# An expert layer on one core: features formed turned, with the weights standing in the array

## The chip, the core and the metric

The kernel runs on one core of a Trainium2 chip. The core's engines work at the same time, each on its own queue of instructions in order: TensorE (PE in the profile; its weight loads are listed apart as PEld), VectorE (DVE), ScalarE (ACT), GpSimd (POOL), and SyncE (SP), whose queue here only starts transfers. ScalarE and GpSimd start transfers too. Transfers from all queues share the core's 16 DMA engines. Matmuls read their operands from SBUF and write to PSUM, which has eight banks of 512 f32 values on each of 128 partitions; SBUF is the larger on-chip memory.

A matmul has one operand that *stands* in TensorE's array (loaded by an LDWEIGHTS instruction) and one that *moves* through it, a column at a time. All data are f32. An ordinary f32 product shows in the profile as two weight loads and two matmuls, a transpose as one of each.

The metric is the time of one execution in device microseconds, as the median of several runs. The kernel before takes 764.09 us (runs of 763.78, 764.09 and 767.37).

## The reference

The input is x of 4 x 1024 tokens with 256 features, and a context of 77 rows for each of the four sequences. Cross-attention comes first, then a mixture of experts:

```python
def swiglu(x, w1, w2, w3):
    return jax.nn.silu(x @ w1) * (x @ w3) @ w2
...
scores = jax.nn.softmax(xf @ Wg, axis=-1)             # 4096 tokens, 32 experts
weights, indices = jax.lax.top_k(scores, TOP_K)       # 4 experts a token
...
for e in range(E):
    ...                                               # the tokens that chose e, at most C of them
    out = swiglu(xf[tok], W1[e], W2[e], W3[e]) * w[:, None]
    y = y.at[tok].add(out)
z = swiglu(xf, Ws1, Ws2, Ws3)                         # the shared expert, all tokens
return (y + z).reshape(B, S, D)
```

An expert has W1 and W3 of 256 x 128 and W2 of 128 x 256; the shared expert's hidden width is 256. The input is added to each of the two layers' results.

## The kernel before

**Stages.** After loading and preparing weights, the kernel runs attention over 32 tiles of 128 tokens (up to about 400 us), with the routing of each block of 512 tokens behind it. Each normalised token row, with its routing numbers, is scattered to a table `xr` in DRAM, once for each expert that the token chose. Then come the expert tiles (about 449 to 720 us), and a tail in which the results are gathered, added and stored.

**An expert tile** is 128 rows of one expert, taken from `xr`. There are 144 in this run, numbered j: 128 (`NM_`) in a main loop and 16 (two lots of eight, the number read at run time) in the body of a `tc.Switch`. Which expert a tile belongs to is only known at run time: a table in SBUF holds it, `registers` (line 1083) loads eight entries at a time into registers of an engine, and `ev[j]` is tile j's expert in TensorE's registers. All experts' weights lie in SBUF in one array `we`, 768 columns an expert: for each half k of the 256 inputs 128 columns of W1 and 128 of W3, and then 256 columns of W2.

**The steps of a tile** are four functions, `steps` in line 1249. In round j of the loop, `expert_in` runs for tile j, `expert_mid` for tile j-1, `expert_turn` for j-2 and `expert_out` for j-3:

- `expert_in` (L1156): two transposes on TensorE turn the rows (PSUM bank `pgT`), VectorE copies them to `gT`, inputs down, tokens across.
- `expert_mid` (L1165): for each k, `gT` stands and 256 columns of `we` move (W1 and W3 side by side), which gives the bank `peh`, tokens down and 2 x 128 features across. ScalarE takes the Silu of the first half to `h` (L1176), VectorE multiplies it by the second (L1177).
- `expert_turn` (L1180): a transpose on TensorE turns `h` (bank `phT`), and ScalarE copies it to `ehT` (L1184).
- `expert_out` (L1187): `ehT` stands, W2 moves, bank `py`; ScalarE scales the rows by their routing weights into `y` (L1196), and GpSimd scatters the 128 rows to their places in `ys` in DRAM (L1197).

**Work around the tiles.** `fetch` (L1101) brings eight tiles' rows on SP's queue, seven rounds ahead, and loads the registers. `take` (L1216) brings back, for 128 tokens, the four results each, once those are scattered, and `add_taken` adds them on VectorE, a step a round. The shared expert runs on blocks of 512 tokens, `shared_in` (two halves), `shared_mid`, `shared_out`, `shared_add` (L581 to L634), placed between the tiles and in the tail; a block's turned rows come from DRAM (`xnd`) by `fetch_shared` (L575) into a tile `sx` of 512 KB. In the tail, six `gather` calls of 1 MB each run on SP's queue (`gy`), and the blocks 3, 4 and 5 of the shared expert are done between the additions and stores.

**What sets the order.** Within `as_written` each engine's instructions keep the order of the program text; nothing is reordered between engines' queues by a planner. A tile pool with `bufs=n` gives a name n buffers in turn, and an instruction that writes a buffer waits until the readers of its previous contents are done. PSUM banks are handed out in turn from one pool of eight. The pool `bp` holds the expert tiles' buffers, two of each name unless said otherwise; `sxp` holds `sx`, three of them.

Of the kernel before, what the change touches and what calls it, by code (L numbers as in the profile page):

```python
# [9 lines left out]
F32 = mybir.dt.float32  # L10
I32 = mybir.dt.int32
U32 = mybir.dt.uint32
AF = mybir.ActivationFunctionType
# [17 lines left out]
def kernel(  # L31
# [65 lines left out]
    def bank(name):  # L97
        return ps.tile([P, 512], F32, tag="bank", name=name)
# [982 lines left out]
    sxp = ctx.enter_context(tc.tile_pool(name="sxp", bufs=3, side="right"))  # L1081
# [14 lines left out]
    ev, groups = [], {}  # L1096
# [4 lines left out]
    def fetch(j):  # L1101
# [10 lines left out]
        ev.extend(registers(e_tab, jt, mybir.EngineType.PE, NE - 1))  # L1112
        groups[j // RG] = [g]
# [41 lines left out]

    def expert_in(j, _):  # L1156
        g = groups[j // RG][0]
        pt = bank(f"pgT_{j}")
        for k in range(KC):
            nc.tensor.transpose(pt[:, k * P : (k + 1) * P], g[:, j % RG, k * P : (k + 1) * P], ident)  # L1160
        gT = bp.tile([P, KC, P], F32, tag="gT", name=f"gT_{j}")
        nc.vector.tensor_copy(gT.rearrange("p k t -> p (k t)"), pt[:, :D])  # L1162
        return gT

    def expert_mid(j, gT):  # L1165
        ph = bank(f"peh_{j}")
        for k in range(KC):
            nc.tensor.matmul(  # L1168
                ph[:, : 2 * H],
                gT[:, k, :],  # L1170
                we[:, ds(ev[j] * EW + k * 2 * H, 2 * H)],
                start=(k == 0),
                stop=(k == KC - 1),
            )
        h = bp.tile([P, H], F32, tag="h", name=f"h_{j}")
        nc.scalar.activation(h, ph[:, :H], AF.Silu)  # L1176
        nc.vector.tensor_tensor(h, ph[:, H : 2 * H], h, ALU.mult)  # L1177
        return h

    def expert_turn(j, h):  # L1180
        pt = bank(f"phT_{j}")
        nc.tensor.transpose(pt[:, :P], h, ident)  # L1182
        hT = bp.tile([P, P], F32, tag="ehT", name=f"ehT_{j}")
        nc.scalar.copy(hT, pt[:, :P])  # L1184
        return hT
# [63 lines left out]
    steps = [expert_in, expert_mid, expert_turn, expert_out]  # L1249
# [5 lines left out]
    with as_written():  # L1255
        fetch(0)
        fetch_shared(1, nc.sync)
        for j in range(NM_ + len(steps)):
            if j % RG == 1 and j + RG - 1 <= NM_:
                fetch(j + RG - 1)  # L1260
            if j in (4 * RG + 4, 5 * RG + 4, 6 * RG + 4):
                fetch_shared(j // RG - 2, nc.sync)
# [47 lines left out]
            if j == NM_ + 2:  # L1310
                fetch_shared(5, nc.scalar)
    assert not adds
    ahead = groups[NM_ // RG][0]
    for n in tc.Switch(more, (NJ - NM_) // RG + 1, hint="more"):
        end = NM_ + n * RG
# [3 lines left out]
        del ev[NM_ + RG :]  # L1319
# [135 lines left out]
```

## Time and profile before

| | |
|---|---|
| median of three runs | 764.09 us |
| the profiled execution | 762.74 us |
| its span, first to last instruction | 761.0 us |
| mean granted TensorE clock | 0.989 of full |
| TensorE matmul busy | 720.0 us |
| VectorE, ScalarE, GpSimd busy | 478.2, 402.3, 404.1 us |
| features `peh` (L1168): 576 matmuls | 150.7 us busy |
| output `py` (L1192): 288 matmuls | 86.1 us busy |
| turning the rows `pgT` (L1160): 288 | 55.1 us busy |
| turning the features `phT` (L1182): 144 | 39.3 us busy |
| bytes moved by DMA | 111.98 MB |

The span has 1.74 us around it that belong to the execution but to no instruction. A group of the profile has its line, engine, operation, what is written from what (`peh<-we,gT`), and the count; then the busy time of the group (overlaps counted once), the mean duration of one, and the idle time of its engine ahead of them with what ended it. Matmuls are pipelined: the mean duration of one `peh` matmul is 385 ns, while two of them start about 217 ns apart. Shapes are partitions x elements. In a timeline row, `x4` means four such instructions merged, the second column is from the first one's start to the last one's end, and brackets give idle time of the engine and what ended it. The slices are fortieths of the span, some 19 us each.

### The profile page before, as it was taken

The page shows a single profiled execution, that of the slowest core. Times are in us where ns is not written, and L with a number is a line of the kernel's source. Part 1 is how long each engine was busy: PE and PEld are TensorE (multiplying, and loading weights), DVE is VectorE, ACT ScalarE, POOL GpSimd, SP SyncE. Part 2 cuts the span into 40 slices and gives each one's busy share as a digit, 9 for nine tenths or more (in the row PEclk, how much of TensorE's full clock was granted, in tenths as well). Part 3 has the DMA queues.
Part 4 walks back from the last instruction along what each step waited for, and adds up shares of the span by engine and source line. Part 5 has one row for each costly group of instructions (what it writes and reads, how often), then busy time and mean ns, then how long its engine had stood idle before and what let it go on. Part 6 is the DMA issues. An engine that isn't in the chain of part 4 may idle for free. (4 is left out here: it accounts for less than half of the span.)

```text
span 761.0 us, 13078 instructions
## 1 busy us (share of the span) xinstructions
PE 720.0 (95%) x3515; PEld 536.6 (71%) x3515; DVE 478.2 (63%) x1368; ACT 402.3 (53%) x1730; POOL 404.1 (53%) x492
## 2 busy tenths in 40 slices
PE   7999999999999999999987779999999999999996
PEld 5866777677777767777763457788888887876754
DVE  2965565777877878776757433644545466645766
ACT  2658567666777576766553002455555555544310
POOL 1003343346777878777786655565565555553500
PEclk9999999999999999999998989999999999999999
DMA  8930000402217131513136451555746579847594
GB/s 284 342 113 1 1 1 1 132 7 87 100 59 253 47 127 52 170 59 120 74 97 210 140 189 65 159 173 183 224 161 195 166 262 311 258 127 244 186 342 163
DMA packets 78599, 111.98 MB, mean 147 GB/s; under 512 B 8949, under 2 KB 63667, under 8 KB 78515
## 3 DMA queue, kind: packets, MB, share of 16 engines
q1 hardware_dynamic: 60319, 68.76, 29.4%
q0 software_dynamic: 13056, 36.72, 13.0%
q10 hardware_dynamic: 5140, 5.55, 2.1%
q8 instruction: 32, 0.52, 0.3%
q14 instruction: 52, 0.43, 0.2%
HBM read 62.36 MB, written 48.64 MB: 146 GB/s over the span
## 5 line engine op out<-in xcount | busy, mean ns | idle before, releaser
L327 ACT ACTIVATE p<-sc,mx 128x77 f32<-128x77 f32 x512 | 159.5, 352 | 93.2 <-DVE mx L319 93.2
L1197 POOL DMA_INDIRECT ys<-y,place x144 | 138.9, 964 | 124.1 <-ACT y L1196 102.0
L1168 PE MATMUL peh<-we,gT 128*128 x576 | 150.7, 385 | 6.9 <-DVE gT L1162 5.4
L378 PE MATMUL po<-we,pT 128*128 128x256 f32 (+1 forms) x640 | 147.3, 383 | 4.8 <-DVE pT L365 3.4
L555 POOL DMA_INDIRECT xr<-xn,row x128 | 128.1, 1000 | 41.1 <-issue 33.1
L342 POOL TENSOR_TENSOR p<-p,su 128x385 f32<-128x385 f32 (+1 forms) x96 | 91.1, 974 | 97.5 <-DVE su L337 76.5
L311 PE MATMUL sc<-we,qT 128*128 128x385 f32 (+1 forms) x384 | 138.9, 509 | 0.9 <-POOL qT L297 0.9
L378 PEld LDWEIGHTS po<-we,pT 128*128 128x128 f32 (+1 forms) x640 | 118.4, 190 | 27.1 <-DVE pT L365 5.8
L327 ACT ACTIVATION_READ_ACCUMULATOR p<-sc,mx 128x1 f32 x512 | 119.3, 233 | 0.0
L1168 PEld LDWEIGHTS peh<-we,gT 128*128 128x128 f32 x576 | 99.2, 192 | 16.7 <-DVE gT L1162 6.5
L311 PEld LDWEIGHTS sc<-we,qT 128*128 128x128 f32 x384 | 71.1, 189 | 54.3 <-issue 27.7
L1176 ACT ACTIVATE h<-peh 128x128 f32<-128x128 f32 x144 | 40.0, 278 | 116.0 <-PE peh L1168 76.3
L1177 DVE TENSOR_TENSOR h<-peh,h 128x128 f32<-128x128 f32 x144 | 41.9, 291 | 87.1 <-ACT h L1176 80.2
L1192 PE MATMUL py<-we,ehT 128*128 x288 | 86.1, 381 | 0.0
L1196 ACT ACTIVATE y<-py,own 128x256 f32<-128x256 f32 x144 | 68.3, 475 | 17.8 <-PE py L1192 2.0
L319 DVE TENSOR_REDUCE mx<-sc 128x5 f32<-128x385 f32 (+1 forms) x96 | 54.3, 576 | 32.8 <-PE sc L311 30.1
L1162 DVE COPY gT<-pgT 128x256 f32<-128x256 f32 x144 | 60.5, 420 | 19.5 <-PE pgT L1160 9.1
L1160 PE MATMUL pgT<-ident,g 128*128 128x128 f32 x288 | 55.1, 274 | 1.3 <-DMA g<-xr 0.5
L1160 PEld LDWEIGHTS pgT<-ident,g 128*128 128x128 f32 x288 | 40.1, 142 | 17.2 <-issue 2.3
L1192 PEld LDWEIGHTS py<-we,ehT 128*128 128x128 f32 x288 | 43.6, 191 | 11.6 <-issue 0.8
L589 PE MATMUL ph<-sx,ws 128*128 128x512 f32 x96 | 46.0, 628 | 1.6 <-DVE y L1236 1.0
L360 PEld LDWEIGHTS pp<-ident,p 128*128 128x128 f32 x320 | 36.1, 139 | 11.4 <-issue 5.5
(227 smaller groups left out, 927.3 us busy)
## 6 DMA issues: line engine op xcount, KB each, us to landing
g<-xr SPq DMA_DIRECT2D x144, 136.0 KB
gx<-ys SPq DMA_DIRECT2D x20, 512.0 KB
gy<-ys SPq DMA_DIRECT2D x6, 1024.0 KB
xr<-y SPq DMA_DIRECT2D x1, 4352.0 KB
y<-in_x SPq DMA_DIRECT2D x8, 512.0 KB
xnd<-xnT SPq DMA_DIRECT2D x6, 512.0 KB
we<-in_W SPq DMA_DIRECT2D x8, 384.0 KB
out<-y ACTq DMA_DIRECT2D x12, 256.0 KB
```

Source lines behind the costliest of these rows:

```text
L311: nc.tensor.matmul(sc[:, : (h1 - h0) * SK], qTs[blk][:, k, o : o + P], mq[:, b, k, h0 * SK : h1 * SK], start=(k == 0), stop=(k == KC - 1),)
L319: nc.vector.tensor_reduce(mx[:, h0:h1], sv, AX.X, ALU.max, negate=True)
L327: nc.scalar.activation(probs[t][:, h, :], sv[:, h - h0, :], AF.Exp, bias=mx[:, h : h + 1], accum_out=su[:, h : h + 1],)
L342: nc.gpsimd.tensor_tensor(p[:, h0:h1, :], p[:, h0:h1, :], su[:, h0:h1].unsqueeze(2).to_broadcast([P, h1 - h0, SK]), ALU.mult,)
L378: nc.tensor.matmul(po[:, :D], pT[:n, i, :], vo[b][:n, i, :], start=(i == 0), stop=(i == KT - 1))
L555: sct = nc.gpsimd.indirect_dma_start(out=xr, out_offset=bass.IndirectOffsetOnAxis(ap=row[:, i : i + 1], axis=0), in_=xn[:, c, :], in_offse ...
L1160: nc.tensor.transpose(pt[:, k * P : (k + 1) * P], g[:, j % RG, k * P : (k + 1) * P], ident)
L1162: nc.vector.tensor_copy(gT.rearrange("p k t -> p (k t)"), pt[:, :D])
L1168: nc.tensor.matmul(ph[:, : 2 * H], gT[:, k, :], we[:, ds(ev[j] * EW + k * 2 * H, 2 * H)], start=(k == 0), stop=(k == KC - 1),)
L1192: nc.tensor.matmul(py[:, :D], hT, we[:, ds(ev[j] * EW + KC * 2 * H, D)], start=True, stop=True)
L1196: nc.scalar.activation(y, py[:, :D], AF.Identity, scale=own[:, i, 1:2])
L1197: sent = nc.gpsimd.indirect_dma_start(out=ys, out_offset=bass.IndirectOffsetOnAxis(ap=place_[:, i : i + 1], axis=0), in_=y, in_offset=None,)
```

## The change

The features are formed turned. In `expert_mid` the experts' weights now stand in the array, a block of 128 x 128 at a time, and `gT` moves: for each of W1 and W3 (f) and each half k of the inputs there is a product of 128 moving columns. The bank `peh` then holds features down and tokens across, W1's in columns 0 to 127 and W3's in 128 to 255. Silu and product therefore write `ehT` directly, and the transpose, the bank `phT`, its copy and the buffer `h` are gone; `ehT` has three buffers. The third step only passes its tile on, so the output of a tile stays in the same round.

The standing weights are read from a fixed place: a new function `weigh` copies the tile's 512 columns of W1 and W3 on ScalarE from `we`, at an offset from ScalarE's own registers (`eva`, loaded in `fetch` beside `ev`), to a tile `w` of two buffers. The first two tiles of the main loop and of the Switch body are copied in `expert_in`; every other tile's copy stands in `expert_mid` of the tile two before, behind the Silu. `last` keeps the main loop from copying for tiles of the Switch body. W2 is still read from `we` in `expert_out`.

To make room, `sxp` has two buffers instead of three, and the loads of the shared blocks move: block 4 is loaded where block 5 was (after the main loop, on ScalarE's queue), and block 5 in the tail, on ScalarE's queue behind `shared_in(3, 1)`.

```diff
-    sxp = ctx.enter_context(tc.tile_pool(name="sxp", bufs=3, side="right"))
+    sxp = ctx.enter_context(tc.tile_pool(name="sxp", bufs=2, side="right"))
...
         ev.extend(registers(e_tab, jt, mybir.EngineType.PE, NE - 1))
+        eva.extend(registers(e_tab, jt, mybir.EngineType.Activation, NE - 1))
...
+    fixed, last = {}, [NM_]
+
+    def weigh(j):
+
+        fixed[j] = bp.tile([P, KC * 2 * H], F32, tag="w", name=f"w_{j}")
+        nc.scalar.copy(fixed[j], we[:, ds(eva[j] * EW, KC * 2 * H)])
+
     def expert_in(j, _):
         g = groups[j // RG][0]
+        if j % NM_ < 2:
+            weigh(j)
...
     def expert_mid(j, gT):
+
+        w = fixed.pop(j)
         ph = bank(f"peh_{j}")
-        for k in range(KC):
-            nc.tensor.matmul(
-                ph[:, : 2 * H],
-                gT[:, k, :],
-                we[:, ds(ev[j] * EW + k * 2 * H, 2 * H)],
-                start=(k == 0),
-                stop=(k == KC - 1),
-            )
-        h = bp.tile([P, H], F32, tag="h", name=f"h_{j}")
-        nc.scalar.activation(h, ph[:, :H], AF.Silu)
-        nc.vector.tensor_tensor(h, ph[:, H : 2 * H], h, ALU.mult)
-        return h
-
-    def expert_turn(j, h):
-        pt = bank(f"phT_{j}")
-        nc.tensor.transpose(pt[:, :P], h, ident)
-        hT = bp.tile([P, P], F32, tag="ehT", name=f"ehT_{j}")
-        nc.scalar.copy(hT, pt[:, :P])
+        for f in range(2):
+            for k in range(KC):
+                nc.tensor.matmul(
+                    ph[:, f * P : (f + 1) * P],
+                    w[:, (2 * k + f) * H : (2 * k + f + 1) * H],
+                    gT[:, k, :],
+                    start=(k == 0),
+                    stop=(k == KC - 1),
+                )
+        hT = bp.tile([P, P], F32, tag="ehT", name=f"ehT_{j}", bufs=3)
+        nc.scalar.activation(hT, ph[:, :P], AF.Silu)
+        nc.vector.tensor_tensor(hT, ph[:, P : 2 * P], hT, ALU.mult)
+        if j + 2 < last[0]:
+            weigh(j + 2)
+        return hT
+
+    def expert_rest(j, hT):
+
         return hT
...
-    steps = [expert_in, expert_mid, expert_turn, expert_out]
+    steps = [expert_in, expert_mid, expert_rest, expert_out]
...
-            if j in (4 * RG + 4, 5 * RG + 4, 6 * RG + 4):
+            if j in (4 * RG + 4, 5 * RG + 4):
                 fetch_shared(j // RG - 2, nc.sync)
...
             if j == NM_ + 2:
-                fetch_shared(5, nc.scalar)
+                fetch_shared(4, nc.scalar)
...
-        end = NM_ + n * RG
+        end = last[0] = NM_ + n * RG
...
-        del ev[NM_ + RG :]
+        del ev[NM_ + RG :], eva[NM_ + RG :]
...
         shared_in(3, 1, AF.Silu)
+        fetch_shared(5, nc.scalar)
```

More of the change, by code (lines that the diff above doesn't have):

```diff
@@ L1095 @@
     bp = bp_stack.enter_context(tc.tile_pool(name="bp", bufs=2, reuse_waits="tile"))
-    ev, groups = [], {}
+    ev, eva, groups = [], [], {}
     def table(j):
```

## The prediction, made before the result was known

> **What bounds the kernel now.** I read the page's busy shares and slices first, to see which engine is the bound and where.
>
> ```profile
> span 761.0 us, 13078 instructions
> PE 720.0 (95%) x3515; PEld 536.6 (71%) x3515; DVE 478.2 (63%) x1368; ACT 402.3 (53%) x1730; POOL 404.1 (53%) x492
> PE   7999999999999999999987779999999999999996
> DMA  8930000402217131513136451555746579847594
> ```
>
> TensorE is busy 95% of the span, and nearly without a hole from slice 25 to slice 39; the expert tiles run in most of these (about 449 to 720 us). The DMA engines are close to full in slices 33 to 35 and again in slice 39, the tail. So time is won only by shortening TensorE's own work per tile, and it is kept only where no transfer ends last. Next the costliest groups, for what one expert tile issues (x144 tiles).
>
> ```profile
> L1168 PE MATMUL peh<-we,gT 128*128 x576 | 150.7, 385 | 6.9 <-DVE gT L1162 5.4
> L1176 ACT ACTIVATE h<-peh 128x128 f32<-128x128 f32 x144 | 40.0, 278 | 116.0 <-PE peh L1168 76.3
> L1196 ACT ACTIVATE y<-py,own 128x256 f32<-128x256 f32 x144 | 68.3, 475 | 17.8 <-PE py L1192 2.0
> L1160 PE MATMUL pgT<-ident,g 128*128 128x128 f32 x288 | 55.1, 274 | 1.3 <-DMA g<-xr 0.5
> ```
>
> An ordinary product in f32 is two weight loads and two matmuls (576 for 288 in the text), a transpose one of each (288 for 288). The idle column shows that TensorE hardly waits. What a step costs TensorE is not its mean duration, which overlaps the next, but the distance between starts. The chain of waits gives that, here in a stretch where it runs along TensorE.
>
> ```profile
> 709.70 0.87 PE peh L1168 x4
> 710.56 0.11 PE phT L1182
> 710.67 0.43 PE py L1192 x2
> 711.11 0.22 PE pgT L1160 x2
> 711.32 0.86 PE peh L1168 x4
> 712.19 0.11 PE phT L1182
> 712.30 0.43 PE py L1192 x2
> ```
>
> A tile takes 1.63 us: 0.87 for the features (peh), 0.11 for turning them (phT), 0.43 for the output (py), 0.22 for turning the rows (pgT). The same 1.63 us separates every two tiles in the timeline around 520 us. Features plus turn run 709.70 to 710.67 and 711.32 to 712.30: 0.97 and 0.98, mean 0.975.
>
> **TensorE's part of the change.** The turn goes: one transpose, 0.11 us. The four matmuls of 256 moving columns (0.217 us each) become eight of 128 moving columns, each with its own load of 128x128 f32 weights. The columns streamed are the same; the question is whether twice as many loads still hide. The trace has that shape once per block: line 519, f32, full weights, 128 moving columns, loads and matmuls alternating. The groups by shape, then the timeline:
>
> ```profile
> L519 PE MATMUL pf<-mask,tri 128*128 128x128 f32 x16 | 3.2, 280 | 0.1
> L519 PE MATMUL pf<-cum,ones 128*128 128x128 f32 x16 | 3.1, 275 | 0.0
> ```
>
> ```profile
> 408.28 0.39 PE L519 MATMUL pf<-cum,ones 128*128 128x128 f32 x2
> ```
>
> Two matmuls of 275 ns fill 0.39 us, so the second starts 0.112 us after the first (3.1 us / 8 pairs = 0.388, less 0.275). Transposes, also 128 columns, stand 0.11 apart in the chain (0.109 by 0.38 us for two of 273 ns), with a shorter load (142 against 192 ns by mean). Eight steps therefore cost 0.872 (at 0.109) to 0.896 us (at 0.112). I take 0.111, since every second step, from one product to the next, is nearer the transposes' distance: 0.888 us. Gain per tile 0.975 - 0.888 = 0.087 us, by 144 tiles 12.5 us; ends 11.4 and 14.8 us. Line 519 shows only four steps in a row; that is what is unproven. If the loads did not hide at all, a step would cost the load's 192 ns: 1.536 - 0.975 = 0.56 us a tile, 81 us lost, the far end.
>
> [...]
>
> The address arithmetic for the feature weights (two register operations a tile on TensorE's queue, 51 to 55 ns each) goes too. It ran about 0.8 us ahead of the matmuls, so it gains nothing.
>
> **ScalarE's part.** It loses the copy of the turned features (260 ns) and gets a copy of 128x512 from SBUF to SBUF. No row has that. Below: 0.64 us, the 128x512 copies out of PSUM (L365). Above: 0.84 us, the 128x256 normalisation from SBUF with two pointers (589 ns, L247) plus 256 columns at the 0.98 ns between the 260 and 638 ns copies. I take 0.70, the PSUM copy and the 50 to 65 ns by which a 128x128 from SBUF (L475, 326) exceeds one from PSUM (260, 278). ScalarE's tile now:
>
> ```profile
> 524.38 0.28 ACT L1176 ACTIVATE h<-peh 128x128 f32<-128x128 f32 x1 [0.61 <-PE peh L1168]
> 524.56 0.26 ACT L1184 COPY ehT<-phT 128x128 f32<-128x128 f32 x1
> 524.93 0.47 ACT L1196 ACTIVATE y<-py,own 128x256 f32<-128x256 f32 x1
> ```
>
> Afterwards 0.28 + 0.70 + 0.47 = 1.45 us in a tile of 1.54, by durations, which overlap by 0.10 (0.18 between the first two starts): about 1.2 us. The new copy waits for the features of the tile two before (its buffer); behind it stands y, for which POOL's scatter waits. It ends about 0.5 us into the next tile and the weights are read 1.2 us after that; y comes some 0.2 us later than now, and POOL (0.96 us a tile) has 0.6 us spare. Price 0. With the cover gone, every nanosecond over a 1.54 us tile is paid 144 times. The 18 register loads on ScalarE (0.59 to 0.82 us each, by TensorE's own) come behind a y and ahead of a Silu that waits anyway: 0, at most 18 x 0.8 = 14 us if nothing covered them.
>
> **VectorE, banks.** The product keeps its 0.29 us and shape. Without the phT bank three banks a tile turn over in eight; the features get a whole tile more before py wants them. Both 0; if that slack failed, TensorE would stand as it did for phT, 1.0 us in all.
>
> **The moved transfers.** Blocks of 512 KB for the shared expert: block 4 goes from SP's queue at tile 52 to ScalarE's, where block 5's was issued (687.4; block 4 is first read at 729), 0. SP has one issue (0.46 us) less there. Block 5 is now issued in the tail, by ScalarE, when the second half of block 3's features has been read: about 729.5 us. It is needed at about 739.5, four stages later. The engines are full of the gathers then (0.41 MB per us); sharing evenly with them it takes 0.5 MB / 0.2 = 2.6 us, after the 4 us that the store issued at 727.77 waited for its first packet: landed at about 736. Queued behind it on ScalarE are store(4) and the next Silu, due 731.1; neither is late. Price 0; the far end, behind all gathers (744.5 us), is 5 to 6 us.
>
> **What takes gain back.** In the Switch body the second lot of rows waits for a chain that the edit does not shorten (tile 127's scatter, three takes, then the lot, landing at 702.6, with TensorE already idle for 0.55 and 0.78 us): the gain of the first eight tiles there, 8 x 0.087 = 0.7 us, turns into waiting. From 610 to 670 us the DMA share is already this high, with TensorE hardly idle:
>
> ```profile
> 640.00:650.00 10.00, 10.00 (x56) 8.33 (x55) 6.94 (x24) 5.38 (x18) 5.64 (x6) 1.00 0.91 292
> ```
>
> Tiles 6% closer (1.63 / 1.54) make 0.96 of it. Of the 36 tiles or so there, worth 3.1 us, I take 0.7 as lost; ends 0 and 3.1.
>
> **Sum.** -12.5 + 0.7 + 0.7 = -11.1 us. The profiled execution took 762.74 us (span 761.0 and 1.74 around it): it would be 751.6. The median before is 764.09, 1.35 above the profiled one; on that, 753.0.
>
> **Rivals.**
> Waits eat more: block 5 late by 5 us, or the full 3.1 us of the DMA stretch with the step at 0.112 us. For it: DMA shares over 0.9 and a full tail. Against: 3 us of slack in the tail. Time 753.0 + 4 to 7 = 757 to 760.
> The narrow loads don't hide in a long stream (the other side): one nanosecond a step costs 8 x 144 = 1.15 us. [...] For it: loads of 192 ns in steps of 111, and fewer than five such steps in a row in the trace. Against: their spacing did not grow over these.
> ScalarE becomes the bound: starts 0.18 + copy + 0.37 have to pass 1.54 us, so the copy would need 1.0 us; 1.07 cancels the gain, and at 1.2 us the tile is 1.75, 0.12 over now: 17 us slower, 781. Against: the far row is 0.84.
> [...]
>
> **How the numbers follow.** About 0.5% (3.8 us) is what a measurement here can tell from no change: 760.3 to 767.9. Forecast 0.70 (its own range 749 to 757); waits eat more 0.12; within half a percent 0.05; slower 0.13 (narrow loads 0.10, ScalarE 0.03). The first two are faster: 0.82. The range goes from 749.0 (14.8 us gained, nothing lost) to 760.3, and leaves out the last two cases.
>
> **What would show it.** In the chain, peh x8 at 0.87 to 0.90 and tiles 1.52 to 1.55 apart around 520 us; no phT; the copy on ScalarE at 0.64 to 0.84 us, with TensorE never waiting for it past the first tiles; the wait before tile 136 longer by 0.7 us; no idle TensorE ahead of block 5 in the tail. Wrong, if peh's steps stand over 0.12 us apart, or TensorE waits for the weights' copy in each tile.

## The result, and the profile after

The changed kernel takes 770.12 us (median of seven runs, 767.61 to 773.19), the kernel before 763.73 beside it (seven runs, 760.69 to 767.37): a ratio of 1.0091, with a 95% interval from 1.0067 to 1.0115. It is 0.9% slower, where 753.0 us had been forecast. The page of the changed kernel, in the lines that answer to those of before:

```profile
span 768.3 us, 13673 instructions
PE 713.5 (93%) x3947; PEld 547.2 (71%) x3947; DVE 476.4 (62%) x1368; ACT 437.4 (57%) x1730; POOL 403.7 (53%) x492
PE   7999999999999999999987689999899988899996
...
L1181 PE MATMUL peh<-gT,w 128*128 128x128 f32 x1152 | 155.2, 278 | 21.2 <-DVE gT L1172 13.6
...
L1189 ACT ACTIVATE ehT<-peh 128x128 f32<-128x128 f32 x144 | 39.9, 277 | 99.4 <-PE peh L1181 54.0
L1162 ACT COPY w<-we 128x512 f32 x144 | 88.3, 613 | 2.2 <-PE ph L589 1.1
```

TensorE is busy for less time than before, 713.5 against 720.0 us, in a longer span. It now waits: 21.2 us of idle time stand ahead of `peh`, where it was 6.9, and the slices with an 8 lie among the expert tiles. Measured from the first product of tile 0 to that of tile 143, the tiles took 260.3 us before (453.9 to 714.2) and take 269.2 now (454.0 to 723.2).

Yet where TensorE does not wait, a tile is as short as forecast. The chain of waits of the changed kernel, in its Switch body (start, length, what):

```profile
720.46 0.89 PE peh L1181 x8
721.35 0.43 PE py L1204 x2
721.79 0.22 PE pgT L1170 x2
722.01 0.89 PE peh L1181 x8
```

The features take 0.89 us and the tile 1.55. So the gain is there in each tile, and something gives it back between them. The timeline of TensorE, ScalarE and VectorE around one such place, 522 to 527 us:

```profile
522.91 1.06 PE L1181 MATMUL peh<-gT,w 128*128 128x128 f32 x8
523.80 0.60 PE L1204 MATMUL py<-we,ehT 128*128 x2
524.24 0.38 PE L1170 MATMUL pgT<-ident,g 128*128 128x128 f32 x2
524.46 1.06 PE L1181 MATMUL peh<-gT,w 128*128 128x128 f32 x8
...
526.73 1.02 PE L1181 MATMUL peh<-gT,w 128*128 128x128 f32 x7 [0.57 <-DVE gT L1172]
```

```profile
523.14 0.48 ACT L1208 ACTIVATE y<-py,own 128x256 f32<-128x256 f32 x1
525.66 0.28 ACT L1189 ACTIVATE ehT<-peh 128x128 f32<-128x128 f32 x1 [2.04 <-PE peh L1181]
525.83 0.61 ACT L1162 COPY w<-we 128x512 f32 x1
```

```profile
525.97 0.29 DVE L1190 TENSOR_TENSOR ehT<-peh,ehT 128x128 f32<-128x128 f32 x1 [1.99 <-ACT ehT L1189]
526.17 0.41 DVE L1172 COPY gT<-pgT 128x256 f32<-128x256 f32 x1
```

The eight products that end at 523.97 fill the bank that the Silu of 525.66 reads. ScalarE stands idle for 2.04 us for TensorE's signal, though by TensorE's own rows the work has been over for 1.69 us. The Silu comes late, so VectorE's product comes late, so the copy of the next tile's rows behind it comes late (526.17), and TensorE waits 0.57 us for that copy. The raw updates of TensorE's semaphore show the same from the other side: those for work that ended at 523.97, 524.40 and 524.62 are recorded at 525.635, 525.678 and 525.720, 42 to 43 ns apart. A usual one comes 14 ns after the end. I call a tile late when its Silu starts more than 0.3 us after its last feature product has ended: 46 of the 144 tiles are late after the change, 3 before. In 25 of the 46 ScalarE had stood idle since the products ended, so the signal itself was late, by up to 2.57 us; in most of the others ScalarE was still busy with work that earlier late signals had put off. ScalarE's signals were on time: in the 120 tiles in which VectorE had stood waiting for the Silu, its product starts 33 ns or less after the Silu's end.

The tail is as forecast. The chain there has no idle TensorE ahead of block 5 of the shared expert:

```profile
731.37 8.82 PE ph L589 x20
740.19 3.45 PE pz L617 x16
743.65 6.87 PE ph L589 x16
750.51 3.45 PE pz L617 x16
753.97 3.45 PE ph L589 x8
```

### The profile page after: what moved, and what is told of

It is laid out like the page before. It is cut to its first block, busy times and chain, and to the rows that moved or that the text cites. A ratio compares the mean times of both kernels' runs of the same rounds, so it can differ in the third digit from the quotient of the medians.

```text
span 768.3 us, 13673 instructions
## 1 busy us (share of the span) xinstructions
PE 713.5 (93%) x3947; PEld 547.2 (71%) x3947; DVE 476.4 (62%) x1368; ACT 437.4 (57%) x1730; POOL 403.7 (53%) x492
## 5 line engine op out<-in xcount | busy, mean ns | idle before, releaser
L1181 PE MATMUL peh<-gT,w 128*128 128x128 f32 x1152 | 155.2, 278 | 21.2 <-DVE gT L1172 13.6
L1181 PEld LDWEIGHTS peh<-gT,w 128*128 128x128 f32 x1152 | 139.9, 191 | 29.4 <-ACT ehT L1189 8.4
L1190 DVE TENSOR_TENSOR ehT<-peh,ehT 128x128 f32<-128x128 f32 x144 | 41.8, 290 | 98.3 <-ACT ehT L1189 68.0
L1189 ACT ACTIVATE ehT<-peh 128x128 f32<-128x128 f32 x144 | 39.9, 277 | 99.4 <-PE peh L1181 54.0
L1162 ACT COPY w<-we 128x512 f32 x144 | 88.3, 613 | 2.2 <-PE ph L589 1.1
```

The lines of the kernel that those rows point to most:

```text
L1162: nc.scalar.copy(fixed[j], we[:, ds(eva[j] * EW, KC * 2 * H)])
L1181: nc.tensor.matmul(ph[:, f * P : (f + 1) * P], w[:, (2 * k + f) * H : (2 * k + f + 1) * H], gT[:, k, :], start=(k == 0), stop=(k == KC - 1),)
```

## The experiments

The first theory was density: a tile now has 24 loads and matmuls on TensorE in 1.55 us, where it had 18 in 1.63, and the signals come late because TensorE issues more than whatever passes its signals on can take. The rivals were ScalarE (its copies, its register loads, the moved transfers) and a mere delay that a longer pipeline would hide.

The runs soon showed something that none of these had foreseen: the kernel before itself took two different times, 746 to 747 us in some measurements and 759 to 766 in others. The table puts all runs of the real kernel beside the time of before in the same measurement; the rows are told one by one below. Tile pitch is the distance of tiles 24 and 127 divided by 103 (some work of the shared expert lies in it).

| run | before, beside it | ratio (95%) | tile pitch | late tiles |
|---|---|---|---|---|
| before, first profile | 763.7 | | 1.66 us | 3 |
| b1_before_again | 766.1 | | 1.66 | 4 |
| the change, first profile | 763.7 | 1.0091 (1.0067 to 1.0115) | 1.76 | 46 |
| a1_after_again | 766.1 | 1.0181 (1.0143 to 1.0219) | 1.83 | 61 |
| a2_after_third | 763.3 | 1.0065 (1.0043 to 1.0087) | 1.71 | 42 |
| a3_after_fourth | 765.9 | 1.0216 (1.0169 to 1.0262) | 1.79 | 53 |
| **a4_after_fifth** | **746.9** | **0.9827 (0.9800 to 0.9854)** | **1.56** | **1** |
| e1_scalar_work | 746.9 | 1.0040 (1.0026 to 1.0053) | 1.64 | 0 |
| e2_narrow_no_copy | 746.9 | 0.9846 (0.9822 to 0.9870) | 1.56 | 0 |
| e2_narrow_no_copy_2 | 763.3 | 0.9980 (0.9954 to 1.0006) | 1.63 | 25 |
| e3_wider | 746.9 | 1.0169 (1.0138 to 1.0201) | 1.75 | 1 |
| e3_wider_2 | 763.3 | 1.0185 (1.0155 to 1.0216) | 1.77 | 5 |
| e4_deeper | 746.9 | 0.9832 (0.9794 to 0.9870) | 1.59 | 18 |
| e4_deeper_2 | 766.1 | 1.0129 (1.0090 to 1.0167) | 1.84 | 108 |
| e6_more_transfers | 765.9 | 1.0318 (1.0271 to 1.0366) | 1.87 | 39 |

I call the two the prompt condition (before at 746 to 747 us) and the late condition (before at 759 to 766). The texts written before the runs speak of two kinds of chip; that was a guess, and the last two runs took it away.

### ScalarE's work alone

```diff
+        w = bp.tile([P, 2 * H], F32, tag="w", name=f"w_{j}")
+        nc.scalar.copy(w, we[:, ds(eva[j] * EW, 2 * H)])
...
         nc.vector.tensor_tensor(h, ph[:, H : 2 * H], h, ALU.mult)
+        if j + 2 < last[0]:
+            weigh(j + 2)
         return h
```

with the register loads, `sxp` and the moved loads of the change.

> The kernel before, with what the change puts on ScalarE and on the transfers and nothing of what it does to TensorE: each tile's ScalarE also copies weights, two tiles ahead, behind the Silu (256 of the 512 columns, so that ScalarE's time per tile is 1.01 + about 0.4 = 1.4 us, as after the change, where it is 0.61 + 0.48 + 0.28 = 1.37), the register loads for it are made, and the shared blocks' loads stand where the change puts them. Nothing reads the copies. Theory 1 (the denser TensorE instructions are what makes its signals late; 18 loads and multiplies per 1.63 us here as before): Silu stays on time, 762 to 766 us. Theory 2 (ScalarE's longer queue, its register loads or the moved transfers hold the work up): Silu late and TensorE waiting as after the change, 768 us or more.

No tile is late, and the pitch stays at 1.64 us; the copies of 256 columns take 397 ns each. The kernel is 0.4% slower all the same, 2.5 us. In the profiled execution TensorE stands for 3.6 us, in one wait ahead of the tail, for VectorE's additions; but at 752.5 us that was the slowest of ten, so it isn't shown that this wait makes the 2.5 us. In the prompt condition, then, ScalarE's part of the change, with half the columns copied, makes no signal late. It was not run in the late one.

### The narrow products without the copies

```diff
-        fixed[j] = bp.tile([P, KC * 2 * H], F32, tag="w", name=f"w_{j}")
-        nc.scalar.copy(fixed[j], we[:, ds(eva[j] * EW, KC * 2 * H)])
+        fixed[j] = experts[:, j % NE, : KC * 2 * H]
...
-        eva.extend(registers(e_tab, jt, mybir.EngineType.Activation, NE - 1))
```

> The kernel after the change, with the turned features but without ScalarE's copies and its register loads: the weights that stand in the array are taken from a place in the resident table that is known when the program is written (tile j takes expert j mod NE, so the first two products use the wrong expert's weights; the third keeps its own). TensorE's instructions are those of after, 24 loads and multiplies per 1.545 us; ScalarE has 0.76 us of work in a tile. Theory 1 (TensorE's signals come late when its instructions are dense): Silu is still up to 2 us late in bursts and tiles average 1.70 to 1.77 us; without the copy to wait for some of the stalls are gone, total 760 to 772 us. Theory 2 (ScalarE's copy and queue are the cause): tiles of 1.545 us throughout, total 749 to 754 us.

> The narrow products without ScalarE's copies once more (weights from a place known when written, so two of three products use the wrong expert). On a chip of the slower kind: theory 1 (too many TensorE instructions for what passes its signals on there, limit about 13 per us) gives tiles of 1.75 to 1.85 us and a total within 6 us of the changed kernel; if the copies are needed for the trouble, 1.55 us and 15 us or more faster than the changed kernel. On a chip of the faster kind, within 4 us of the changed kernel.

Prompt: 735.1 us, no late tile, 1.56 us a tile. Late: 25 late tiles, 1.63 us a tile, and a ratio of 0.998 whose interval holds 1. Without a single copy on ScalarE the gain is gone in the late condition, so the copies and their registers are not needed for the trouble. They add to it: measured beside it, the full change has 42 late tiles and is 6.2 us slower (767.5 against 761.3). Theory 1 had forecast a pitch of 1.75 to 1.85 there; that was too much.

### Wider products

```diff
-                    ph[:, f * P : (f + 1) * P],
+                    ph[:, 2 * f * P : 2 * f * P + WIDE],
                     w[:, (2 * k + f) * H : (2 * k + f + 1) * H],
-                    gT[:, k, :],
+                    gT.rearrange("p k t -> p (k t)")[:, k * (2 * P - WIDE) : k * (2 * P - WIDE) + WIDE],
```

with `WIDE = 160`, and the product taken from the third block of the bank.

> The kernel after the change with 160 moving columns in place of 128 in each of the eight feature matmuls (32 columns more than is used, the others land beside it; the second half's operand starts 32 columns early, so the features are wrong): the same 24 loads and multiplies per tile, but the tile is 8 x 0.024 = 0.2 us longer by TensorE, 1.74 us, 13.8 instructions per us. ScalarE's and VectorE's instructions are those of after. Theory 1 (density, a limit near 13.6 per us): Silu nearly on time (lateness summed over the tiles under 20 us, 55 after the change), hardly a stall before peh, total 764 to 772 us, within 0.5% of after although 144 x 0.2 = 28 us of work were added. Theory 2 (ScalarE is what is late, or the lateness is a fixed delay): stalls as after on top of the longer tiles, 778 to 798 us.

> The changed kernel with 160 moving columns for 128 in the feature products once more (the added columns land beside the features; the second half's operand starts 32 columns early). On a chip of the slower kind, theory 1 gives tiles of 1.74 to 1.85 us as in the changed kernel, a total within 8 us of it although 28 us of TensorE's work were added; if the late signals are a fixed delay, it is 15 us or more slower than the changed kernel. On a chip of the faster kind it is 20 to 26 us slower than the changed kernel.

The same instructions, spread over a longer tile. In the late condition only 5 tiles are late, where the change beside it had 42, and the 28 us of added work (8 steps by 0.024 us, which is 0.136 less 0.112 us in m_dense, by 144 tiles) cost 775.5 - 767.5 = 8.0 us. In the prompt condition they cost 758.8 - 734.4 = 24.4 us (from two measurements in which before took the same 746.9). TensorE's waits in the tiles of the late run, 505 to 680 us, beside those of the change in its first profile (in all, times, longest):

```profile
PE peh L1182 <- DVE gT L1173: 1.3, 2, 1.1
PE peh L1182 <- issue: 0.3, 1, 0.3
```

```profile
PE peh L1181 <- DVE gT L1172: 10.7, 15, 2.0
PE peh L1181 <- ACT ehT L1189: 2.8, 3, 1.2
```

So the late signals go with how short the tile is: 5 late tiles in this form and 42 in the change, whose pitches in the prompt condition are 1.75 and 1.56 us. ScalarE's and VectorE's instructions are the same in both kernels, but in the longer tile they too stand further apart, so this run doesn't tell TensorE's density from that of all engines together.

### A deeper pipeline

```diff
-    steps = [expert_in, expert_mid, expert_rest, expert_out]
+    steps = [expert_in, expert_rest, expert_mid, expert_rest, expert_out]
...
-        if j + 2 < last[0]:
-            weigh(j + 2)
+        if j + 3 < last[0]:
+            weigh(j + 3)
```

with three buffers each for `w` and `gT`, four for `y` in place of six, and one in place of two for four small names of the routing.

> The kernel after the change with one tile more between the steps: the turn of a tile's rows is made two tiles ahead of the features instead of one, weights are copied three tiles ahead, with three buffers for each (the scattered rows keep four buffers in place of six for room). If signals are only late by up to 2 us, and catch up by themselves, a tile more of slack (1.54 us) hides most of it: stalls before peh under 6 us (21 after), total 752 to 758 us. If TensorE's signals fall behind because there are too many instructions for what passes them on, more slack only lets it fall behind further: total 765 to 772 us, with Silu later than after (3 us and more).

> The deeper pipeline again (turn two tiles ahead, copies three tiles ahead), now beside the changed kernel on one chip. If late signals are what cost the changed kernel its gain, and there are none here, the deeper one gains nothing on it: within 0.3% of it, 731 to 737 us. If some stalls remain that a tile of slack hides, it is 3 to 6 us faster than the changed kernel; in the condition of the first profiles, 10 us and more.

Prompt: 733.0 us, no better than the change (734.4). Its 18 late tiles stand behind another wait, for the four buffers of `y`: 5.5 us of waiting for scatters from 505 to 690 us. Late: 1.0129, beside 1.0181 for the change beside it (775.4 and 779.9 us), and 108 late tiles whose delays add up to 222 us where the change has 76. In 31 of the 108 ScalarE stood idle until TensorE's signal came; in 75 it had no idle time ahead of the Silu and was working off a backlog. Its longest wait for `peh` grew from 2.3 to 3.4 us. The slack of a tile lets TensorE run further ahead of its readers; then it stalls at another place:

```profile
PE py L1204 <- DVE ehT L1190: 13.2, 20, 0.9
```

A fixed delay of some 2 us would, as an estimate, mostly have been hidden by a tile more of slack (1.54 us). Measured beside each other, the change and its deeper form come out alike, 24 instructions of TensorE's in 1.83 and 1.84 us, 13 per us, which looks like a rate that something can keep up. The other late runs do not bear one rate out: the same 24 instructions took 1.71 to 1.79 us in the other late runs of the change and 1.63 without the copies, 13.4 to 14.7 per us. (Before has 18 at 1.66, 10.9 per us; the wider form 24 at 1.77, 13.6, with few late tiles.) A rate is not shown.

### Both kernels again

> The changed kernel again, unchanged, beside the kernel before on one chip. In the runs e1 to e4 the kernel before takes 746.9 us and not 763.7, and no burst of late TensorE signals is in any of the four traces, while both first profiles have them (from 450 us on) and lack part of the signals' records. Theory 1 (the late signals belong to the condition the first two profiles were taken in, and cost the denser kernel more): here no bursts, tiles of 1.545 us throughout, stalls before peh under 6 us, total 732 to 738 us, 0.980 to 0.988 of before. Theory 2 (the change itself makes signals late, by the copies and the narrow products together): bursts as in the first profile, 750 to 756 us, 1.005 to 1.012 of before.

> The kernel before, unchanged, for its trace beside that of the changed kernel on one chip. Theory 1: no bursts of late signals after 400 us (five in the first profile), expert tiles of 1.63 us, 745 to 749 us, and the 14.6 us that TensorE idled between 400 and 450 us in the first profile are 4 to 5 us. Theory 2: the difference of 17 us to the first profile lies in the granted clock (0.989 there), spread evenly over the stages.

> The changed kernel once more, for comparison on whichever chip this is. The two chips seen so far differ: on one (kernel before 746.9 us) no run of narrow products shows a late signal of TensorE, on the other (766.1) the changed kernel and its deeper form have 40 to 50 bursts of them. Theory 1 (a property of the chip, or of how it is recorded, that costs denser TensorE work more): where the kernel before takes about 747 us, this takes 733 to 738 and shows no burst; where it takes 762 to 768, this takes 768 to 781 with bursts. Theory 2 (chance from run to run, not chip): bursts and time do not go with the time of before.

> The changed kernel, for comparison on whichever chip this is. On a chip where the kernel before takes about 747 us: 733 to 738 us, no burst of late TensorE signals. Where it takes 762 to 768 us: 766 to 781 us, 20 bursts or more after 440 us.

> The changed kernel, for comparison on whichever chip this is; the four seen with it so far were all of the slower kind (before 763 to 766 us). There: 766 to 783 us, 40 to 60 of 144 tiles whose Silu starts more than 0.3 us after its products have ended. On a chip of the faster kind (before about 747): 730 to 738 us, 0.978 to 0.988 of before, no late tile, since there the narrow products without copies took 735.1, the deeper form 733.0, and the form with 160 columns 758.8, which less 144 x 0.2 us is 730.

Three of the four repeats of the change fell in the late condition, with 42 to 61 late tiles and ratios from 1.0065 to 1.0216. The fourth fell in the prompt one: 734.37 us against 746.90, which is 12.5 us less. Its page and chain:

```profile
span 732.6 us, 13673 instructions
PE 702.5 (96%) x3947; PEld 544.2 (74%) x3947; DVE 477.9 (65%) x1368; ACT 439.2 (60%) x1730; POOL 404.1 (55%) x492
...
L1181 PE MATMUL peh<-gT,w 128*128 128x128 f32 x1152 | 153.4, 276 | 6.0 <-DVE gT L1172 2.6
```

```profile
564.10 0.43 PE py L1204 x2
564.53 0.22 PE pgT L1170 x2
564.75 0.89 PE peh L1181 x8
565.64 0.43 PE py L1204 x2
566.08 0.22 PE pgT L1170 x2
566.29 0.89 PE peh L1181 x8
```

Six microseconds of idle time ahead of `peh` in place of 21.2, tiles 1.54 us apart without a hole, and one late tile. ScalarE's Silu now starts 0.03 us after the products end:

```profile
508.48 0.28 ACT L1189 ACTIVATE ehT<-peh 128x128 f32<-128x128 f32 x1 [0.39 <-PE peh L1181]
```

(the products that it waits for are the eight from 507.39 to 508.45). The tiles take 247.4 us from tile 0 to 143, where the first profile of the same program has 269.2; the other 14 us between the two lie ahead of tile 0, which starts at 440.1 in place of 454.0.

The kernel before, again in the late condition, looks as in its first profile: 4 late tiles, 1.66 us a tile. Its granted clock is 0.987; the change had 0.995 in the prompt run and 0.984 to 0.988 in the late ones, which is at most 1.1% where the time differs by 4.5% and more. In the late condition TensorE idles 14.5 us from 400 us to tile 0 in the kernel before, against 4.3 us for e1 in the prompt one. There the same sign is seen on large matmuls. A bank of `ph` is done by 431.4 us (and VectorE, for which the reader also waits, by 433.3), and the activation that reads it starts at 435.31, 0.02 us after a recorded update of TensorE's semaphore; the largest wait, 6.0 us ahead of `pz`, ends after updates at 445.14 to 445.33 for products that ended at 440.1. So the lateness is older than the change and is part of what the kernel before loses in this condition; the change adds to it.

### More transfers

```diff
+        for i in range(2):
+            nc.sync.dma_start(spare[(2 * j + i) % 64 * 16 : ((2 * j + i) % 64 + 1) * 16, :], y[:16, :16])
```

behind each tile's scatter, in the kernel before.

> The kernel before, with two small transfers more in each tile (16 rows of 64 bytes of the tile's scaled rows, to a place in DRAM that nothing reads), TensorE's work unchanged. Each transfer adds 16 updates of a semaphore. Theory 3 (on some chips what fails is the sum of all engines' instructions and of the transfers' updates: on the faster chip some 28 instructions and 27 updates per us are recorded in the expert tiles, on the slower ones 24 and 7 to 13, the transfers' updates being mostly lost): on a chip of the slower kind TensorE's signals now come late here too, 15 bursts or more after 500 us and 6 us or more over before; on a chip of the faster kind within 2 us of before. Theory 1 (TensorE's own instructions alone are too many): no bursts, within 3 us of before on either chip.

It is 24 us slower than before, with 39 late tiles, as theory 3 (the sum of all engines' instructions and the transfers' updates is too much) had it. But ScalarE's waits from 505 to 680 us name another cause first:

```profile
ACT y L1197 <- DMA spare<-y: 21.6, 12, 4.6
ACT h L1177 <- PE pgT L1161: 20.1, 11, 2.1
```

The buffers of `y` waited for the added transfers, which stand in order on SP's queue behind the fetches. That alone holds ScalarE for 21.6 us and makes Silus late. Late signals are there as well (the second line), but the experiment can't say which of the two cost the time. It is inconclusive.

### Bare products

Four kernels were made of nothing but dense f32 products, whose banks a VectorE copy reads, without and with company.

```python
for i in range(each):
    nc.tensor.matmul(pt[:, :cols], w[:, i, :], m[:, :cols], start=(i == 0), stop=(i == each - 1))
nc.vector.tensor_copy(s, pt[:, :16])
for _ in range(copies):        # on three engines
    ...
for _ in range(small):
    nc.sync.dma_start(spare[...], s)
if scatter and g % scatter == 0:
    nc.gpsimd.indirect_dma_start(...)
```

> The disputed effect by itself: a kernel with nothing but f32 products of standing 128x128 weights, in stretches of 256, 160, 128, 112, 96, 128 and 64 moving columns, each bank of 8 products (2 in the second stretch of 128) read by one small VectorE copy, and stretches of 512 columns between for a backlog to drain. It computes nothing of the reference. On a chip of the faster kind: copies follow the last product by the same 0.1 us or less in all stretches, and a product takes its columns at the clock (0.111 us at 128). On a chip of the slower kind, theory 1: at 256 columns (18.4 loads and multiplies per us) or fewer the copies fall behind by more with each bank until TensorE waits for a free bank, and from there every stretch of up to 160 columns runs at the same 13 loads and multiplies per us, 0.30 us for a product of four, whatever its columns. If the limit is on signals and not on instructions, the second stretch of 128 (four times the signals) is much slower than the first.

Measured beside the change with its 42 late tiles (before at 763.3), no copy starts more than 0.22 us after its bank's last product, with 18 loads and matmuls per us for 86 us on end. Density of TensorE's instructions by itself, the first theory, falls with this. The run also settles the step of the prediction that was unproven. Groups by shape (busy time, mean ns):

```profile
L41 PE MATMUL c<-m,w 128*128 128x128 f32 x768 | 85.9, 275 | 0.0
L41 PE MATMUL d<-m,w 128*128 128x112 f32 x768 | 85.9, 275 | 0.0
L41 PE MATMUL e<-m,w 128*128 128x96 f32 x768 | 85.9, 275 | 0.0
```

768 matmuls in a row, each with its own load, take 85.9 us: 0.112 us a step at 128 columns, and exactly as much at 112 and at 96.

> The disputed effect by itself, now with company (nothing of the reference is computed): banks of 8 products of 128 columns, each bank read by a VectorE copy, in stretches alone, with one or two small transfers of 128 rows per bank, with two of 16 rows, with a 504 KB transfer every four banks, with three small copies each on ScalarE and GpSimd per bank, with 256 columns and two transfers, and with both transfers and copies; stretches of 512 columns between. The first such kernel, with TensorE's products alone at 18 loads and multiplies per us, showed no copy more than 0.22 us late on a chip where the changed kernel had 25 bursts. Theory 3: on a chip of the slower kind the copies come late, by 0.5 us and more, in the stretches with two small transfers per bank (36 updates per us), whatever their rows, and in those with copies and transfers, not in the one with large transfers (4.5 updates per us). If it is the bytes moved that disturb, it is the stretch with large transfers alone. On a chip of the faster kind nothing is late anywhere.

In the late condition (before at 765.9) nothing is late in any stretch, either. The doses of transfers were half of what the text says, since a bank of eight f32 products takes 1.79 us and not 0.89: 21 instructions with 19 updates per us; and the copies on ScalarE and GpSimd all ran at the start, not in their stretches.

> Dense products of 128 columns once more (nothing of the reference is computed), now with the other engines kept to the pace of the banks: per bank of 0.89 us two small copies each on ScalarE, VectorE and GpSimd; those and two small transfers; a scatter by GpSimd of 128 rows of 1 KB every second bank alone; scatter and copies; all three; and all three with 256 columns (half the products); stretches of 512 columns between. Theory 3 (sum of all engines' instructions and updates): on a chip of the slower kind VectorE's copy of a bank comes 0.5 us and more late in the stretch with all three, hardly or not where one is missing, and not with 256 columns. If GpSimd's scatter, whose writes are in every stretch where a signal has been late, is what disturbs, it comes late in every stretch with the scatter and in none without. If neither is late, what disturbs is not in this kernel. On a chip of the faster kind nothing is late.

> Dense products with company again, at higher doses (nothing of the reference is computed; a bank of 8 products of 128 columns takes 1.79 us, since each f32 product is two passes). Per bank: three copies each on three engines (some 28 instructions and 6 updates per us); four small transfers alone (21 and 38); two transfers, two copies each and a scatter every second bank (27 and 27, the expert tiles' own mixture); four transfers and three copies each (31 and 42); the same with 4 products of 256 columns in that time (22 and 42); four transfers, three copies and the scatters (32 and 46). The expert tiles have 27 and 27 after the change and 24 and 26 before; on a chip of the faster kind the last such kernel, up to 27 and 27, showed no late signal. Theory 3 (the sum, with a limit between the 40 per us that m_mixed reached without harm on a slower chip and the 54 of the changed kernel): on a chip of the slower kind VectorE's copy of a bank comes 0.5 us and more late with four transfers and copies (73) and with the mixture (54) and everything (78), perhaps with transfers alone (59), not with copies alone (34). If it is the number of instructions alone (24 to 25 per us is where the changed kernel stays on the slower chips), late with copies alone (28) too and not with transfers alone (21). If neither, nothing is late here: then what disturbs is not in this kernel. On a chip of the faster kind nothing is late.

Both fell in the prompt condition (746.9 and 745.8). In the first, no copy starts more than 0.54 us after its bank's last product. In the second, copies come up to 4.5 us late in the stretches with four transfers a bank, where the transfers read the copy's buffers; that the transfers hold these for so long was not shown, and the stretches say nothing of signals.

> One program of two parts, so that the last run tells something in either condition. First the kernel before with two small transfers more in each tile, as in e6_more_transfers (there 24 us slower than before, 39 tiles with a late Silu). Then, after its last store, the stretches of m_company, 40 banks each: products of 128 columns with copies (23 instructions and 4 updates per us), copies and transfers (26 and 22), scatters (20 and 6), copies and scatters (24 and 9), all three (27 and 27, as in the expert tiles), all three with 256 columns (19 and 28). If the run is in the condition in which the kernel before takes 762 to 768 us: the first part is as in e6_more_transfers; by theory 3 VectorE's copy of a bank is 0.5 us and more late in the stretch with all three and not in the others; if nothing is late there, the sum is not enough, and what disturbs is something that only the whole kernel has. If it is in the condition in which it takes about 747: no late Silu in the first part, which ends within 3 us of where the kernel before ends, so that the 24 us of e6_more_transfers are shown to be the late signals' and not the transfers' own; nothing is late in the second part.

The late condition again (before at 758.7). The first part is as in e6_more_transfers: 29 late tiles, 1.84 us a tile. In the second part, some 400 us after the expert tiles in the same execution, the stretch with all three kinds of company runs at 26 instructions and 21 recorded updates per us with a copy 0.19 us late by median and 0.54 once; it had the same 0.19 and 0.54 in the prompt run of m_company. So at the expert tiles' own rate of instructions, with transfers, copies and GpSimd's scatters, the late condition still leaves bare products' signals on time. Records are missing there too: the same stretch has 26.5 recorded updates per us in the prompt run of m_company. Theory 3 in its plain form, a limit on the sum, is not what these runs show.

**What stays open.** What the late condition is, and what in the whole kernel it needs to make TensorE's signals late. It isn't the chip by its number: two numbers came in both conditions (11 with before at 765.9 and 745.8, 14 at 746.9 and 758.7), some minutes apart. It goes with lost records: TensorE's semaphore has 910 recorded updates in the first profile of the change and 1090 in the prompt one, and from 550 to 600 us the deeper kernel has 10 updates of all semaphores recorded per us in the late run and 27 in the prompt one. The loss begins at about 180 us, behind the first scatter of GpSimd's (177.0 us): in the first profile of the change TensorE's semaphore has 105 updates for 104 instructions from 100 to 177 us, and 119 for 161 from 180 to 300. But the late tiles do not go with the number of records lost: the kernel before has 842 recorded updates for 1245 of TensorE's instructions that make one, and 3 late tiles, the change 910 for 1101, and 46. No run here was made without records, so whether the recording causes the late signals or only suffers with them wasn't settled. One rival was left untested: in the bare products with company TensorE makes 0.56 signals per us, in the changed kernel's tiles 1.7 to 1.9. The one bare stretch with as many (banks of two products, 2.2 per us) had no company; there a copy was 0.22 us late at most.

## Why the prediction was right or wrong

**TensorE's step was right.** Eight narrow steps were put at 0.888 us; the chain has 0.89, and 768 in a row run at 0.112 us. The gain of 0.087 us a tile, 12.5 us by 144 tiles, is also what separates the two kernels in the prompt condition: 746.90 - 734.37 = 12.5 us. That the two agree to a tenth is partly luck. No trace of the kernel before was taken in the prompt condition; e1, the nearest to it, takes 257.5 us from tile 0 to 143 in its one profile where the change takes 247.4, so 10.1 us lie in the tiles, and the rest elsewhere.

**The step that failed** is the cover by ScalarE and VectorE, put at nothing: "Price 0" for ScalarE, with its sign "TensorE never waiting for it past the first tiles", and "Both 0" for VectorE and the banks (1.0 us if that slack failed). The prediction counted the time from the end of the features to the next use of each buffer by durations, and took TensorE's signal to come at the end of its work. In the late condition it comes up to 2.57 us later, and 46 tiles of 144 are late. The slack that was named (the copy ends 0.5 us into the next tile, the weights are read 1.2 us after) is smaller than that. The idle time ahead of `peh` rose from 6.9 to 21.2 us, 14 us, and 13.6 of the 21.2 end with VectorE's copy of the turned rows, which the second zero covers. The tiles as a whole lost 269.2 - 247.4 = 21.8 us against the prompt run; by the starts of the feature matmuls, 19.6 of these lie ahead of and between them. What makes the signals late stays open.

The profile of before held a hint: 3 tiles late in this way, and ahead of the tiles, from 400 us to tile 0, TensorE idled 14.6 us. The largest wait there (4.6 us ahead of `pz`) hangs on the same kind of chain: VectorE stood until 434.67 us for a product (`pf`, L519) whose matmuls had ended at 428.59. The prediction read the idle column of the tiles' groups alone and found that "TensorE hardly waits"; it did not ask why an engine's waits ended later than the work that they waited for.

**ScalarE's copy** takes 613 ns, a little under the lower bound of 640, and starts of ScalarE's instructions leave it room; ScalarE did not become the bound. One wait for the copies came in both conditions and stood in no term: at the first tile of the Switch body, whose weights are copied only there, TensorE waits 1.59 us in the changed kernel and 0.69 in the kernel before, 0.9 us. **Moved transfers:** block 5 came in time, price 0, right. **The second lot** in the Switch body was to be waited for 0.7 us longer; the gap ahead of it is 1.30 us in the prompt run, and was 0.55 + 0.78 = 1.33 before: the term was not there. **The DMA stretch** was given 0.7 us: in the prompt run TensorE idles 0.7 us from tile 90 to 127, so that much at most, but the total came out 12.5 us shorter, so nothing of the two terms is seen in the sum. The range's lower end, 14.8 us under 764.09, is 749.3 and not 749.0.

**The rivals.** "Waits eat more" had the right kind and the wrong place and size: it looked for 4 to 7 us in the DMA stretch and the tail, at 757 to 760. The narrow loads did hide: 768 steps in a row ran at 0.112 us each (m_dense). The kernel did become slower, but not for either of the two reasons that were given for that. No rival had the mechanism, since each took a finished product to be known at once to its reader.

## What to carry to other kernels

Before pricing an edit at nothing because other work covers it, look in the trace at how late a reader starts after its producer has ended, not only at whether the bound engine idles; where a few tiles already start late (here 3 of 144), slack worked out from durations isn't there. A tile made shorter on the bound engine spends the slack of the chains beside it: here 1.55 us in place of 1.63, and in the late condition 46 late tiles in place of 3. And where the kernel before has two times, decide in both: here the same edit is 1.7% faster in one and 0.7 to 2.2% slower in the other, and no version tried beats the kernel before in both.

## What the runs showed of the hardware that was not expected

- In m_dense an f32 step of load and matmul takes 0.112 us at 128, 112, 96 and 64 moving columns alike, a floor in this range (64: 1024 matmuls in 114.5 us); at 160 it is 0.136 and at 256 0.220.
- TensorE's signals can come late, in some runs and not in others of the same program: in the expert tiles up to 2.57 us after its rows end (the change, first profile), ahead of them once 6.1 us (428.59 to 434.67 us in the kernel before). The updates that follow come in bursts, mostly 42 to 43 ns apart (in the first profile of the change 81 of the 105 gaps under 0.1 us).
- The same program took 734.4 or 767 to 782 us with a granted clock of 0.984 or more in every profile.
